# A bidirectional recurrent stack on one core: the first pair of items reordered, the fold of gamma and beta moved into other slots, late norms allowed to catch up

## The chip, the core and the metric

The kernel runs on one core of one Trainium2 chip. A core has TensorE (PE, matrix products and transposes into PSUM), VectorE (DVE), ScalarE (ACT), GpSimd (POOL) and SyncE (SP, which issues most DMAs here). Each engine works through its own queue in order and waits on semaphores for the others. The metric is the device time of one execution in microseconds; lower is better.

## The reference, cut to what matters

For each of B = 8 items, x is 512 tokens by 512 features. Layer norm, then a stack of four layers in two directions (the backward one over the reversed tokens, with the same weights), a fusion with a residual, then a feed-forward block with ternary weights and another residual:

```python
def _mingru(x, Wz, bz, Wh, bh):              # here Wz = Wh and bz = bh
    z = sigmoid(einsum('bsi,hi->bsh', x, Wz) + bz)
    h_tilde = tanh(einsum('bsi,hi->bsh', x, Wh) + bh)
    a = clip(1.0 - z, CLAMP_LO, CLAMP_HI)
    return _linear_scan(a, z * h_tilde)       # h[t] = a[t] * h[t-1] + b[t]

def _stack(x, ...):
    h = x
    for i in range(4):
        h_new = _mingru(h, Wz[i], bz[i], Wh[i], bh[i])
        if i > 0:
            h_new = h_new + h
        h = _layernorm(h_new, gamma, beta)
    return h

x = x + einsum(concat(stack_fwd(ln(x)), stack_bwd(ln(x))), fusion_W) + fusion_b
x = x + ffn(ln(x))     # W_fc and W_proj reduced to -1, 0, 1 by the mean of their magnitudes
```

The last layer's gamma and beta need not be applied to the states: fusion_W can be multiplied by gamma, the mean can be taken out of its rows, and beta's part goes into the bias. The kernel calls that the fold.

## The kernel before, in words

**Tiles.** The recurrent state of one item and direction lies with features on partitions: four chunks of 128 features by 512 tokens (`xT[b]`, `h_bd`). A layer of an item and direction is four *chunks* `u_bd_l_o`: a float32 product of four accumulating matmuls (eight in the trace, 128x512), then on ACT three activations of it (a, t and z; L431 to L433), on DVE the clamp and product (L437, L438), the scan over the tokens (L442) and the residual sum (L497). In the first layer both directions share the product: DVE scales u by the tokens' reciprocal deviation (L464), ACT makes a, t, z, and DVE runs a forward scan into `zf` and a backward scan into `z`.

**Norms.** Layer norm needs tokens on partitions. A *turn* `pt` (L293) is four 128x128 transposes on PE into a PSUM buffer, then statistics on DVE (L149 to L160), the power on POOL (L156), and a scaled copy to a token tile on ACT (`tok`, L166 and L167). After all four turns of a state a *back* `pf` (L302) transposes four token tiles into one chunk of the new state, and ACT copies it out with gamma and beta (L308). PSUM holds four buffers for u (`ps_u`), two for turns (`ps_t`) and two for backs (`ps_f`); a tile's buffer is free again after its last reader.

**Slots.** The order of work is written out by hand. `slot(work, cap)` issues one piece of PE work (a chunk, or a fusion tile), then what is due: first-layer scalings ("factors"), up to `cap` turns and backs from the queues `turns` and `backs` (`shares`), turns of x or y (`x_shares`), first-layer "scans", the work's own DVE end, "resid" stages, and then the ACT copies of the turns and backs. `now` counts slots. `extra` holds the work on the ternary weights: every second slot in the first pair (absolute values on ACT), every fourth later (comparisons on DVE, L171 and L172, with DMA in and out). `shares` takes a second piece when the slot's cap is 2, or when the piece is late: `late = at + piece < now`.

**Order of the run.** Items go in pairs. Before the loop: loads, statistics of x of item 0, the centring of the first weights (`pm0`), the first layers of items 0 and 1 (`f0`, `f1`). For each pair: layers 1 to 3 over (b,0), (b,1), (b+1,0), (b+1,1), then eight fusion tiles (`pu`, L528) with the next pair's first layers in between. The feed-forward block for all items comes last, from about 1,250 us.

**The fold before.** Behind the first layers two slots of their own form the sums over gamma and beta (`fold_sums`, PE chunk `pfold`, L609); behind (1,0) and (1,1) of layer 1 one slot each multiplies the four chunks of the fusion weights of one direction (`fold`: `pm` L625 on PE, four L630 on DVE), and one more slot adds to the bias (`fold_bias`: `pb` L636, L639).

Waits in the trace carry the line of a helper, so tiles are named here by item, direction, layer and chunk: `pt_10_0_2` is the turn of token block 2 for item 1, direction 0, layer 0.

Of the kernel before, what the change touches and what calls it, by code (L numbers as in the profile page):

```python
# [9 lines left out]
F32 = mybir.dt.float32  # L10
F32R = mybir.dt.float32r
AF = mybir.ActivationFunctionType
ALU = mybir.AluOpType
# [11 lines left out]
def kernel(  # L25
# [89 lines left out]
    warm = const.tile([P, 1], F32, name="warm")  # L115
    nc.vector.memset(warm, 0.0)

    xT[0] = hp.tile([P, NC_, S], F32, tag="h", name="xT_0")
# [4 lines left out]
    for c in range(NC_):  # L123
        (nc.scalar if c % 2 else nc.sync).dma_start(out=xT[0][:, c, :], in_=xt[0][ts(c, P), :])
    load_xT(1)
    for t in range(NT):
        load_x("n", 1, t)
    nc.sync.dma_start(out=gam, in_=gamma)
    nc.sync.dma_start(out=bet, in_=beta)
# [77 lines left out]
    with rec:  # L207
# [28 lines left out]
        def shares(cap):  # L236


            last = []
            for q in (turns, backs):  # L240
                some = []
                for i in range(2):
                    if not q or not ready(q[0][0]):
                        break
                    at, piece = q[0][:2]
                    late = (at.at if isinstance(at, Tokens) else at) + piece < now[0]
                    if i >= cap and not late:
# [39 lines left out]
        def turned(zs, t, name, frees=0):  # L287
            def source():
                if t == NT - 1:
                    zlive[0] -= frees  # L290
                pt = ps_t.tile([P, H], F32, tag="pt", name=f"pt_{name}")
                for c in range(NC_):
                    nc.tensor.transpose(pt[:, ts(c, P)], zs[c][:, ts(t, P)], ident)  # L293
                return pt
            return source
# [20 lines left out]

        def norm(s, zs, tag, pause):

# [125 lines left out]
        def first_layer(b, lag=0):  # L444
# [4 lines left out]
            def chunk(o):  # L449
                def work():  # L450
# [11 lines left out]
                    def scaled():  # L462
# [140 lines left out]


        def fold_sums(d):

            ps = ps_u.tile([P, H], F32, tag="u", name=f"pfold_{d}")
            for c in range(NC_):
# [3 lines left out]
                )  # L612

            def end():
                folded[d] = tokp.tile([P, H], F32, tag="tok", name=f"fold_{d}")
                held[0] += 1
                nc.scalar.copy(folded[d], ps)
            return end

        folded = {}  # L620

        def fold(d):

            pm = ps_u.tile([P, H], F32, tag="u", name=f"pm_{d}")
            nc.tensor.matmul(pm, lhsT=picks[1], rhs=folded[d], start=True, stop=True)  # L625

            def end():
                for c in range(NC_):
                    w = fw[:, d * NC_ + c, :]
                    nc.vector.scalar_tensor_tensor(w, w, gam[:, c : c + 1], pm, ALU.mult, ALU.subtract)  # L630
            return end

        def fold_bias():
            pb = ps_u.tile([P, H], F32, tag="u", name="pb")
            for d in range(2):
                nc.tensor.matmul(pb, lhsT=picks[0], rhs=folded[d], start=(d == 0), stop=(d == 1))  # L636

            def end():
                nc.vector.tensor_tensor(fb, pb, fb, ALU.add)  # L639
                held[0] -= 2  # L640
            return end

# [17 lines left out]
        take(xbacks)()  # L660
        both = const.tile([P, NC_, 2, 64], F32, name="both")
        picks = []
        for i in range(2):
            s = const.tile([P, P], F32, name=f"fpick{i}")
            nc.vector.memset(s, 0.0)
            nc.vector.memset(s[64 * i : 64 * i + 1, :], 1.0 / H if i else 1.0)
            picks.append(s)
        f0, f1 = first_layer(0), first_layer(1, 2)
        for work in f0:
            slot(work, 2)  # L670
        for i, v in enumerate((bet, gam)):
            nc.vector.tensor_copy(both[:, :, i, :], v.unsqueeze(2).broadcast_to([P, NC_, 64]))
        for work in f1:
            slot(work, 2)
        for d in range(2):
            slot(lambda d=d: fold_sums(d), 2)
        for b in range(0, B, 2):
# [13 lines left out]
            for l in range(1, L):  # L691
# [5 lines left out]
                for s in ((b, 0), (b, 1), (b + 1, 0), (b + 1, 1)):  # L697
# [258 lines left out]
```

## Time and profile before

| | us |
|---|---|
| median of 3 runs | 1767.56 |
| lowest and highest | 1766.42, 1767.7 |
| the profiled execution | 1769.31 |
| its span, first to last instruction | 1767.3 |
| busy: PE, DVE, ACT, POOL | 1721.4, 1451.1, 1066.2, 214.5 |

A busy share is an average over all stages. In the page's 40 slices (44 us each) PE is busy for 90% or more from the fourth slice on to the last but one, and its clock is granted at nine tenths or more in each slice; what happens inside the first 160 us is seen in windows of 20 us and in the timelines. The matrix products here are float32. PE's rows in a timeline overlap a little, since matmuls are pipelined; durations between starts are the safer measure.

### The profile page before, as it was taken

How to read it: one execution, taken by the hardware profiler on the slowest of the kernel's cores; microseconds unless marked ns; L12 is line 12 of the kernel's file. 1: busy time of each engine (PE TensorE's matmuls, PEld its weight loads, DVE VectorE, ACT ScalarE, POOL GpSimd, SP SyncE). 2: the span in 40 equal slices, each digit the busy share in tenths (PEclk: the TensorE clock that was granted, in tenths of full speed). 3: DMA queues.
4: the chain of work that ended last, by engine and by line, in shares of the span. 5: the costliest groups of instructions: out<-in, count | busy, mean ns of one | idle time of the engine just before them, and what ended most of it. 6: DMA issues, size and time to landing. Idle time of an engine off the chain costs nothing.

```text
span 1767.3 us, 19729 instructions
## 1 busy us (share of the span) xinstructions
PE 1721.4 (97%) x6424; PEld 1046.7 (59%) x6424; DVE 1451.1 (82%) x2865; ACT 1066.2 (60%) x1836; POOL 214.5 (12%) x334
## 2 busy tenths in 40 slices
PE   7989999999999999999999999999999999999998
PEld 3554554455554445555444455554588888888886
DVE  6977989779999977999897799997468778778876
ACT  2887884358886325787632588872156556566653
POOL 1111111111111111111111111111000000000000
PEclk9999999999999999999999999999999999999999
DMA  7002210110231111123101201101301101101100
GB/s 262 12 30 78 96 54 19 48 48 13 72 102 54 28 38 54 36 72 107 49 24 42 96 13 48 59 14 42 126 1 48 38 11 48 49 9 40 48 24 24
DMA packets 46454, 91.73 MB, mean 52 GB/s; under 512 B 5264, under 2 KB 5264, under 8 KB 45328
## 3 DMA queue, kind: packets, MB, share of 16 engines
q1 hardware_dynamic: 45488, 88.91, 14.8%
q10 hardware_dynamic: 864, 1.57, 0.3%
q8 instruction: 50, 0.82, 0.2%
q14 instruction: 52, 0.43, 0.1%
HBM read 65.30 MB, written 25.17 MB: 51 GB/s over the span
## 4 chain that ended last, share of the span: by engine, by line
PE 62%; DVE 29%; issue 6%; ACT 2%; POOL 0%; DVEq 0%; DMA 0%; POOLq 0%; ACTq 0%
PE u L414 16%; PE pu L528 12%; PE ph L782 12%; PE po L809 11%; DVE z L442 7%; DVE st L149 5%; DVE z L438 4%; PE u L457 4%; PE pt L293 3%; DVE z L497 2%; PE pf L302 2%; DVE a L437 2%; DVE mv L151 1%; DVE ve L155 1%; DVE st_x L149 1%
## 5 line engine op out<-in xcount | busy, mean ns | idle before, releaser
L414 PE MATMUL u<-xT,gw 128*128 128x512 f32 x768 | 351.1, 601 | 0.0
L414 PE MATMUL u<-h,gw 128*128 128x512 f32 x768 | 350.7, 600 | 0.0
L442 DVE TENSOR_TENSOR_SCAN z<-a,z 128x512 f32<-128x512 f32 x224 | 274.3, 1224 | 7.8
L149 DVE BATCH_NORM_STATS2 st<-pt 128x6 f32<-128x512 f32 x256 | 177.2, 692 | 71.7 <-PE pt L293 71.2
L786 ACT ACTIVATE g<-ph 128x512 f32<-128x512 f32 x128 | 76.4, 597 | 245.9 <-PE ph L782 245.9
L414 PEld LDWEIGHTS u<-xT,gw 128*128 128x128 f32 x768 | 141.2, 194 | 141.0 <-issue 141.0
L414 PEld LDWEIGHTS u<-h,gw 128*128 128x128 f32 x768 | 141.1, 194 | 140.7 <-issue 140.7
L156 POOL TENSOR_TENSOR rs<-ve,mhalf 128x1 f32<-128x1 f32 x192 | 122.9, 640 | 704.1 <-DVE nmu L160 649.1
L809 PE MATMUL po<-pwq,ghi 128*128 128x512 f32 x512 | 203.6, 398 | 0.0
L809 PE MATMUL po<-pwq,glo 128*128 128x512 f32 x512 | 199.9, 390 | 0.0
L782 PE MATMUL ph<-yhi,fcq 128*128 128x512 f32 x512 | 199.8, 390 | 0.0
L782 PE MATMUL ph<-ylo,fcq 128*128 128x512 f32 x512 | 199.7, 390 | 0.0
L431 ACT ACTIVATE a<-u,ngb 128x512 f32<-128x512 f32 x192 | 131.2, 683 | 99.6 <-PE u L414 98.7
L438 DVE TENSOR_TENSOR z<-z,t 128x512 f32<-128x512 f32 x224 | 153.7, 686 | 16.6 <-ACT z L433 16.6
L167 ACT ACTIVATE tok<-pt,nmr,rs 128x512 f32<-128x512 f32 x192 | 149.2, 777 | 6.4
L797 DVE TENSOR_TENSOR acc<-acc,g 128x512 f32<-128x512 f32 x112 | 77.4, 691 | 91.1 <-ACT g L786 90.1
L433 ACT ACTIVATE z<-u,gb 128x512 f32<-128x512 f32 x192 | 132.6, 691 | 0.0
L431 ACT ACTIVATE a<-z,ngb 128x512 f32<-128x512 f32 x32 | 23.1, 722 | 179.7 <-DVE z L464 179.7
L432 ACT ACTIVATE t<-u,gb 128x512 f32<-128x512 f32 x192 | 131.0, 682 | 0.0
L302 PE MATMUL pf<-ident,tok 128*128 128x128 f32 x768 | 116.8, 276 | 13.0 <-ACT tok L167 10.4
L293 PEld LDWEIGHTS pt<-ident,z 128*128 128x128 f32 x640 | 78.8, 142 | 84.6 <-issue 52.4
L166 ACT ACTIVATE nmr<-nmu,rs 128x1 f32<-128x1 f32 x192 | 56.5, 294 | 107.5 <-POOL rs L156 96.8
(138 smaller groups left out, 2711.0 us busy)
## 6 DMA issues: line engine op xcount, KB each, us to landing
xn<-in_x_dram SPq DMA_DIRECT2D x32, 256.0 KB, 4.6
xf<-in_x_dram SPq DMA_DIRECT2D x32, 256.0 KB, 4.3
x<-xf SPq DMA_DIRECT2D x32, 256.0 KB, 2.0
xy<-x SPq DMA_DIRECT2D x32, 256.0 KB, 4.1
out_dram<-xy SPq DMA_DIRECT2D x32, 256.0 KB, 2.0
xT<-in_xt_dram SPq DMA_DIRECT2D x7, 1024.0 KB, 7.0
fca<-in_fc_wT_dram SPq DMA_DIRECT2D x16, 256.0 KB, 2.9
pwa<-in_proj_wT_dram SPq DMA_DIRECT2D x16, 256.0 KB, 2.7
```

The costliest lines, as they stand in the source:

```text
L149: nc.vector.bn_stats(st, src)
L167: nc.scalar.activation(dst, src, AF.Identity, bias=nmr, scale=rs)
L293: nc.tensor.transpose(pt[:, ts(c, P)], zs[c][:, ts(t, P)], ident)
L302: nc.tensor.transpose(pf[:, ts(t, P)], toks[t][:, ts(c, P)], ident)
L414: nc.tensor.matmul(u, lhsT=gw[l][:, c, ts(o, P)], rhs=h[:, c, :], start=(c == 0), stop=(c == NC_ - 1),)
L431: nc.scalar.activation(a, u, AF.Sigmoid, bias=ngb[:, l, o : o + 1], scale=-1.0)
L433: nc.scalar.activation(z, u, AF.Sigmoid, bias=gb[:, l, o : o + 1])
L438: nc.vector.tensor_tensor(z, z, t, ALU.mult)
L442: nc.vector.tensor_tensor_scan(dst[:, d], a[:, d], z[:, d], 0.0, ALU.mult, ALU.add)
L528: nc.tensor.matmul(pu, lhsT=hs[d][:, c, ts(t, P)], rhs=fw[:, d * NC_ + c, :], start=(c == 0), stop=(c == NC_ - 1),)
L782: nc.tensor.matmul(ph, lhsT=w, rhs=ys[b][c][i], start=(c == 0 and i == 0), stop=(c == NC_ - 1 and i == 1),)
L809: nc.tensor.matmul(po[b][t], lhsT=part[:, ts(t, P)], rhs=pwq[k // NP_][:, k % NP_, :], start=(k == 0 and i == 0), stop=(k == NF - 1 and i ...
```

## The change

- The backward scan of the first layer of item 0 is put off to the "resid" stage of the next slot. Item 1's stay where they were.
- Before the first slot two of item 1's four x statistics are issued; the loads of its x are issued ahead of the load of `xT_1`.
- The slot of item 1's second chunk has a cap of 4: all four turns of item 0's forward norm go into it. The last two of those turns use the `ps_f` buffers. `shares` takes up to `cap` pieces.
- In the first pair's first-layer norms turns and backs are numbered in pairs (`t // pair`, `c // pair`), so that two of them are due per slot.
- A piece counts as late one slot earlier: `<=` for `<`. This holds for all pairs.
- The fold has no slots of its own. `fold_sums(d)` follows (0,0) and (0,1) of layer 1; `fold(d)` follows (0,0) and (0,1) of layer 2 and puts one chunk in each of four slots; `fold_bias` follows (1,0) of layer 2. There are five slots fewer, so the pieces of `extra` meet other chunks.
- The constants of the fold (`both`, `fpick`) are set up at the start.

```diff
     for c in range(NC_):
         (nc.scalar if c % 2 else nc.sync).dma_start(out=xT[0][:, c, :], in_=xt[0][ts(c, P), :])
-    load_xT(1)
     for t in range(NT):
         load_x("n", 1, t)
+    load_xT(1)
...
-                for i in range(2):
+                for i in range(max(2, cap)):
                     if not q or not ready(q[0][0]):
                         break
                     at, piece = q[0][:2]
-                    late = (at.at if isinstance(at, Tokens) else at) + piece < now[0]
+                    late = (at.at if isinstance(at, Tokens) else at) + piece <= now[0]
...
-                pt = ps_t.tile([P, H], F32, tag="pt", name=f"pt_{name}")
+                spare = name.startswith("00_0") and t > 1
+                pt = (ps_f if spare else ps_t).tile([P, H], F32, tag="pf" if spare else "pt", name=f"pt_{name}")
...
-        def norm(s, zs, tag, pause):
+        def norm(s, zs, tag, pause, pair=1):
...
-                queue(turns, s, at, t, tokens(turned(zs, t, f"{tag}_{t}", NC_), toks, None, f"{tag}_{t}"))
+                queue(turns, s, at, t // pair, tokens(turned(zs, t, f"{tag}_{t}", NC_), toks, None, f"{tag}_{t}"))
             for c in range(NC_):
-                queue(backs, s, toks, c, back(toks, dst, c, True, f"{tag}_{c}"))
+                queue(backs, s, toks, c // pair, back(toks, dst, c, True, f"{tag}_{c}"))
...
                             scan(f, a, z, False)
-                            scan(z, a, z, True)
                             zf.append(f)
-                            zb.append(z)
                             if o == NC_ - 1:
                                 state[b, 0] = xT.pop(b)
-                                norm((b, 0), zf, f"{b}0_0", 1)
-                                norm((b, 1), zb, f"{b}1_0", 1)
+                                norm((b, 0), zf, f"{b}0_0", 1, 2 if b < 2 else 1)
+
+                            def backward():
+                                scan(z, a, z, True)
+                                zb.append(z)
+                                if o == NC_ - 1:
+                                    norm((b, 1), zb, f"{b}1_0", 1, 2 if b < 2 else 1)
+                            if b == 0:
+                                stages.append((now[0] + 1, "resid", backward))
+                            else:
+                                backward()
...
-            def end():
-                for c in range(NC_):
+            for c in range(NC_):
+                def chunk(c=c):
                     w = fw[:, d * NC_ + c, :]
                     nc.vector.scalar_tensor_tensor(w, w, gam[:, c : c + 1], pm, ALU.mult, ALU.subtract)
-            return end
+                stages.append((now[0] + c, "resid", chunk))
...
+        for _ in range(2):
+            take(xturns)
         f0, f1 = first_layer(0), first_layer(1, 2)
-        for work in f0:
-            slot(work, 2)
+        for i, work in enumerate(f0 + f1):
+            slot(work, 4 if i == NC_ + 1 else 2)
         for i, v in enumerate((bet, gam)):
             nc.vector.tensor_copy(both[:, :, i, :], v.unsqueeze(2).broadcast_to([P, NC_, 64]))
-        for work in f1:
-            slot(work, 2)
-        for d in range(2):
-            slot(lambda d=d: fold_sums(d), 2)
...
-                    if s[0] == 1 and l == 1:
-                        slot(lambda d=s[1]: fold(d))
-                        if s[1] == 1:
-                            slot(fold_bias)
+                    if b == 0 and l == 1 and s[0] == 0:
+                        fold_sums(s[1])
+                    if b == 0 and l == 2:
+                        if s[0] == 0:
+                            fold(s[1])
+                        elif s[1] == 0:
+                            fold_bias()
```

More of the change, by code (lines that the diff above doesn't have):

```diff
@@ L116 @@
     nc.vector.memset(warm, 0.0)
+    both = const.tile([P, NC_, 2, 64], F32, name="both")
+    picks = []
+    for i in range(2):
+        s = const.tile([P, P], F32, name=f"fpick{i}")
+        nc.vector.memset(s, 0.0)
+        nc.vector.memset(s[64 * i : 64 * i + 1, :], 1.0 / H if i else 1.0)
+        picks.append(s)
     xT[0] = hp.tile([P, NC_, S], F32, tag="h", name="xT_0")
@@ L602, in combined @@
                 nc.vector.tensor_tensor(lo, v, hi.bitcast(F32), ALU.subtract)
+        folded = {}
         def fold_sums(d):
@@ L612, in fold_sums @@
                 )
-            def end():
-                folded[d] = tokp.tile([P, H], F32, tag="tok", name=f"fold_{d}")
-                held[0] += 1
-                nc.scalar.copy(folded[d], ps)
-            return end
-        folded = {}
+            folded[d] = tokp.tile([P, H], F32, tag="tok", name=f"fold_{d}")
+            held[0] += 1
+            nc.scalar.copy(folded[d], ps)
         def fold(d):
@@ L625, in fold @@
             nc.tensor.matmul(pm, lhsT=picks[1], rhs=folded[d], start=True, stop=True)
-            def end():
-                for c in range(NC_):
+            for c in range(NC_):
+                def chunk(c=c):
                     w = fw[:, d * NC_ + c, :]
                     nc.vector.scalar_tensor_tensor(w, w, gam[:, c : c + 1], pm, ALU.mult, ALU.subtract)
-            return end
+                stages.append((now[0] + c, "resid", chunk))
         def fold_bias():
@@ L636, in fold_bias @@
                 nc.tensor.matmul(pb, lhsT=picks[0], rhs=folded[d], start=(d == 0), stop=(d == 1))
[L638 to L641, printed above, removed]
+            nc.vector.tensor_tensor(fb, pb, fb, ALU.add)
+            held[0] -= 2
         def load_pair(use, b):
@@ L660 @@
         take(xbacks)()
[L661 to L667, printed above, removed]
+        for _ in range(2):
+            take(xturns)
         f0, f1 = first_layer(0), first_layer(1, 2)
-        for work in f0:
-            slot(work, 2)
+        for i, work in enumerate(f0 + f1):
+            slot(work, 4 if i == NC_ + 1 else 2)
         for i, v in enumerate((bet, gam)):
             nc.vector.tensor_copy(both[:, :, i, :], v.unsqueeze(2).broadcast_to([P, NC_, 64]))
-        for work in f1:
-            slot(work, 2)
-        for d in range(2):
-            slot(lambda d=d: fold_sums(d), 2)
         for b in range(0, B, 2):
```

## The prediction

> **What bounds the kernel now.** I read the busy shares first, then a table of windows over the first 200 us, then the timelines of TensorE (PE) and VectorE (DVE), and last the chain of work that ended last.
>
> ```profile
> PE 1721.4 (97%) x6424; PEld 1046.7 (59%) x6424; DVE 1451.1 (82%) x2865; ACT 1066.2 (60%) x1836; POOL 214.5 (12%) x334
> ...
> 20.00:40.00 20.00, 16.38 (x46) 7.86 (x45) 19.37 (x35) 6.17 (x9) 2.12 (x4) 0.96 0.69 251
> 40.00:60.00 20.00, 18.80 (x73) 10.21 (x71) 14.91 (x39) 16.80 (x30) 4.59 (x8) 0.95 0.01 1
> ...
> 140.00:160.00 20.00, 16.89 (x57) 8.80 (x56) 14.18 (x34) 12.88 (x26) 2.96 (x5) 0.83 0.09 27
> 160.00:180.00 20.00, 20.00 (x72) 10.50 (x71) 16.98 (x31) 16.69 (x32) 1.97 (x3) 1.00 0.40 135
> ```
>
> A window row gives its length, then busy us of PE, weight loads, DVE, ACT, POOL, then granted clock. PE is the bound over the whole span; only in the first pair is it short of work: 140 to 160 has 3.1 us idle and a clock of 0.83, the next window neither. The PE rows show where:
>
> ```profile
> 37.51 0.77 PE L293 MATMUL pt<-ident,zf 128*128 128x128 f32 x5 [3.51 <-DVE zf L442]
> ...
> 100.31 1.12 PE L302 MATMUL pf<-ident,tok 128*128 128x128 f32 x4 [2.58 <-ACT xT L308]
> ...
> 123.79 2.37 PE L293 MATMUL pt<-ident,z 128*128 128x128 f32 x8 [2.43 <-ACT tok L167]
> ...
> 139.90 3.60 PE L414 MATMUL u<-h,gw 128*128 128x512 f32 x8
> ...
> 151.91 0.48 PE L302 MATMUL pf<-ident,tok 128*128 128x128 f32 x1 [2.62 <-ACT tok L167]
> 152.18 6.42 PE L414 MATMUL u<-xT,gw 128*128 128x512 f32 x8
> ```
>
> Each wait costs its idle time and then a stretch at half clock: the chunk at 152.18 takes 6.42 us, the one at 139.90 takes 3.60 (3.44 from start to start). Idle plus slow work, worked out from the start times of PE's instructions: 3.7+1.8 at 37.5, 2.3+1.7 at 60, 0.6 at 88, 2.7+1.5 at 100, 2.6+1.9 at 124, 0.7 at 149, 2.8+3.0 at 152 and 0.3 at 34: 25.6 us between 13 and 158 us. What DVE does before the last two:
>
> ```profile
> 149.65 2.71 DVE L630 SCALAR_TENSOR_TENSOR fw<-fw,gam,pm 128x512 f32<-128x512 f32 x4
> 152.28 0.69 DVE L149 BATCH_NORM_STATS2 st<-pt 128x6 f32<-128x512 f32 x1
> ...
> 159.08 0.70 DVE L149 BATCH_NORM_STATS2 st<-pt 128x6 f32<-128x512 f32 x1 [4.97 <-PE pt L293]
> ```
>
> The slots that only fold give PE a matmul of 1 us, DVE 2.71 us, and no chunk to cover it. Later the same coupling shows once per pair:
>
> ```profile
> 596.55 1.10 issue
> 597.65 0.68 DVE xT L503
> 598.85 4.86 PE u L414 x8
> ```
>
> Here the quantiser (the "issue" row, its 0.48+0.75 us on DVE) sits just ahead of a residual sum that PE awaits: 3.1 us idle, 1.6 slow; the same at 908.
>
> **Durations.** From the DVE timeline, start to start: scaling M 0.70, product P 1.06, scan S 1.25, residual R 0.70, one norm turn N 1.13 (its token 2.9 after its start: 38.63 to 41.55). A layer slot is P+S+R+N = 4.1 on DVE, and 3.44 + 2 x 0.44 = 4.31 on PE.
>
> **Part by part: the first layer.** The order of the instructions on each engine in the changed program, walked with these durations. Two x1 statistics (1.05 each) move ahead of the first M. Their loads are issued ahead of xT_1's on SP's queue, about 8.2 to 10, and land some 6 us later, when DVE gets there (14.4). xT_1 is issued last of the five; it is first read at 26, so 4 us later costs nothing. The memsets (0.7 us) move into the DMA wait at the start: nothing. With the backward scans a slot behind, zf_0_0_3 ends at 35.9 instead of 37.5. All sixteen transposes of 00_0 follow, but the scale transpose pr_1 now needs a buffer of ps_f, and both hold turns: it waits for tok_00_0_2. DVE runs N from 37.2 (after one backward scan), the third at 39.5, its token at 42.4. So PE idles 4.3 us, u_1_0_2 starts at 43.0 (before: 38.9) and ends, partly slow, at 48.2. Behind it stand pt_01_0_0 and the turns 01_0, queued on DVE ahead of item 1's scaling: DVE idles 1.2 + 4.0 + 2.2 us up to 54. From there DVE has no break: two N (56.3), P S S (59.9), the two copies into both (0.5), M, P S S (64.6), slot 00_1_0 (67.6), M, P S S (71.9), slot 00_1_1 (74.9), P and the forward scan of 1_0_3: 77.2. PE goes u_1_0_3 53.4, u_00_1_0 58.6, and 62.9, 67.2, 70.7 for the next three (chunks of 3.44, groups of four transposes of 0.44 between them), then waits for that scan 6.5 us, and 1.8 slow. pfold_0 ends at 83.2, the chunks of 01_1 at 86.6, 90.9, 96.1, 101.3 (0.4 of waits for token buffers), pfold_1 106.5, u_10_1_0 110.0 (DVE waits 2.4 for it), then 4.31 a slot, once 0.4 for a token behind ACT: u_00_2_0 ends at 146.0. POOL's order stays the same; on ACT scale_1 now stands behind four tokens (1.08 each), which is the 1.2 above. Its losses are 2.9 + 6.3 + 8.6 + 0.8 = 18.6 us. The other way round: before, u_00_2_0 ends at 158.6 with 5.2 us more done (pm, pm, pb, four groups): 158.6 - 5.2 - 146.0 = 7.4. **Gain 25.6 - 18.6 = 7.0 us**, most of it from the waits at 100, 124, 149 and 152.
>
> [...]
>
> **Folding.** The two pfold sums (3.44 each) leave slots of their own, where they covered DVE's scans, for layer 1; pm and pb (0.86, 0.86, 1.72) go to layer 2. PE's sum is unchanged, and the walk contains them. DVE's eight fw pieces (2.71/4 = 0.68 each) go one to a slot of layer 2: 4.1 + 0.68 = 4.8 against 4.31, for eight slots, plus fb 0.68: 6.1 us more on DVE, less 0.2 x 8 of slack, less 3.4 that PE itself gains there. Left: 1.1, and PE waits for the last token of a norm, where I find 0.6 us of slack in the old order. Bounds: 0 (hidden by DVE's tenth of idle between 160 and 250) and 6.1 plus two slow stretches. I take **-1.5**. pm holds one of four ps_u buffers for four slots; three are enough, since a chunk's three ACT readers (2.1 us) end within a slot.
>
> **Five slots fewer.** The quantiser's pieces (1.23 us of DVE, one per four slots) shift by two pieces and to other chunks. In pair two 5 instead of 7 precede the wait at 551 (2.6 us): +1.2. Up to the awaited sum at 598 there are then three instead of two: -1.2; the same at 908: -1.2. Pair four gets two more in layer 1: -0.3. The small threshold steps now fall into layer 3 of pair one, where DVE is late (wait at 294): -0.5. **Sum -2.0.** ACT's absolutes and the fca and pwa loads keep their spacing; they are not waited for.
>
> **Late turns.** With <= and up to two, in the three fusion stages a turn (1.13) moves one slot of 10.75 us earlier, three turns and four backs in each. There PE waits 0.3 + 1.45 (at 661 and 669, and again 971 and 980) for token buffers, with a quantiser piece ahead of those turns; after the shift it is elsewhere. Bounds +2.9 and -3 (one extra N per fusion slot ahead of the sums that free ps_u). I take **+1.0**.
>
> **Sum:** 7.0 - 1.5 - 2.0 + 1.0 = 4.5 us. The profiled execution took 1769.31 (span 1767.3), 1.75 above the median of the runs, so I take it off the median: 1767.56 - 4.5 = 1763.0. Some 0.2%, or 3.5 us, is what a measurement here can tell from no change.
>
> **The rivals.**
> - *The cover is better than I think* (0.15): layer 2 takes fw for nothing, 551 gains and 598 loses less, fusion gains 2: 1759. For it: DVE busy 17.0 of 20 at 160 to 180. Against it: DVE ends the chain all through pair two.
> - *Spent later* (0.12): quantiser and late turns cost 4.5 together; 7.0 - 1.5 - 0.5 - 4.5 = 0.5: 1767. This includes a change without effect.
> - *Folding makes DVE the bound of layer 2* (0.18), slower: if a layer slot has no slack on DVE, its 6.1 us come out as PE waits, two of them long enough for slow work (1.7 each): 9.5 instead of 1.5, with the late turns' +1.0 lost: 7.0 - 9.5 - 2.0 = -4.5: 1772. It decides from the point where P no longer waits for ACT in those slots. For it: 149.65, where 2.71 us on DVE became 2.62 idle and 3.0 slow. Against it: one piece at a time, with a chunk of 3.44 to cover it.
>
> **Chances.** My forecast has 0.55, with its own range 1758 to 1767, of which 0.33 lies below 1764.0 and 0.22 within 0.2%. So faster 0.33 + 0.15 = 0.48, same 0.22 + 0.12 = 0.34, slower 0.18. The range takes in the better rival and most of the third.
>
> **What would show it.** Right: PE idle about 4 us before pr_1 near 42 and about 6.5 before pt_10_0_0 near 77, none over 1 us from 90 to 150, u_00_2_0 finished near 146; a small wait in 180 to 215; the wait at 598 and 908 longer by 1. Wrong: slow work at 100 to 150, waits over 2 us in layer 2, or a first stage where PE doesn't wait for pr_1.

## The result and the profile after

| | us, median | runs | lowest to highest |
|---|---|---|---|
| before | 1767.63 | 10 | 1766.15 to 1769.26 |
| after | 1763.91 | 10 | 1759.61 to 1765.73 |

The ratio is 0.9975, with a 95% interval of 0.9967 to 0.9984: 3.7 us less. On a second chip it was 0.9974 (0.9966 to 0.9982). The profiled execution of after was among the two lowest of its ten: 1759.63 us, span 1757.6, mean granted clock 0.995, where five of the ten had 0.992. That of before stood 1.7 us above its median, at 0.990. So the two spans differ by 9.7 us, and only 3.7 of it is the change in the medians. A second profile of after, from a run nearer its median (label e5_after, span 1762.5, clock 0.992), stands beside it below.

The busy line of the profile page of after:

```profile
PE 1710.4 (97%) x6424; PEld 1042.0 (59%) x6424; DVE 1450.2 (83%) x2865; ACT 1067.4 (61%) x1836; POOL 216.2 (12%) x334
```

The counts are those of before, and PE is still the bound. Its 11 us less of busy time are not less work: most of them, some 9 us by the granted clocks of the two profiles (0.990 of 1767.3 us, 0.995 of 1757.6), are fewer matmuls at half clock. The table of windows (length, busy us of PE, weight loads, DVE, ACT, POOL, then granted clock) shows where the waits of the first pair are now:

```profile
40.00:60.00 20.00, 19.55 (x73) 11.35 (x74) 11.11 (x28) 14.76 (x26) 3.52 (x5) 0.86 0.00 1
60.00:80.00 20.00, 15.15 (x44) 6.95 (x43) 19.55 (x26) 13.24 (x23) 0.00 (x0) 0.91 0.09 26
...
140.00:160.00 20.00, 20.00 (x74) 10.76 (x73) 18.38 (x39) 18.02 (x34) 3.53 (x5) 1.00 0.45 145
```

140 to 160, which had 3.1 us idle at a clock of 0.83, is full at 1.00. What is left of the first pair's waits stands between 34 and 80. PE's timeline there (start, us, what, and in brackets the idle time before it and who ended it):

```profile
33.87 1.64 PE L301 MATMUL pt<-ident,zf 128*128 128x128 f32 x13 [1.54 <-DVE zf L450]
40.45 1.08 PE L352 MATMUL pr<-ident,rx 128*128 128x128 f32 x4 [4.94 <-ACT tok L174]
41.33 5.74 PE L465 MATMUL u<-xT,gw 128*128 128x512 f32 x8
...
62.71 1.32 PE L310 MATMUL pf<-ident,tok 128*128 128x128 f32 x8 [0.97 <-ACT h L316]
75.11 0.77 PE L301 MATMUL pt<-ident,zf 128*128 128x128 f32 x5 [3.87 <-DVE zf L450]
75.71 5.30 PE L626 MATMUL pfold<-fw,both 128*128 128x512 f32 x8
...
140.23 3.60 PE L422 MATMUL u<-xT,gw 128*128 128x512 f32 x8
```

pr_1 waits 4.94 us for a token's release of its buffer, and the chunk behind it runs partly at half clock (5.74 against 3.60). The turn pt_10_0_0 waits 3.87 for the forward scan, and pfold_0 behind it is slow too (5.30). From 95 to 204 us there is no wait over 0.2 us. DVE pays for the buffer as well:

```profile
42.79 0.69 DVE L472 TENSOR_TENSOR z<-u,scale 128x512 f32<-128x512 f32 x1 [1.99 <-ACT scale L356]
47.55 0.70 DVE L156 BATCH_NORM_STATS2 st<-pt 128x6 f32<-128x512 f32 x1 [4.06 <-PE pt L301]
52.73 0.70 DVE L156 BATCH_NORM_STATS2 st<-pt 128x6 f32<-128x512 f32 x1 [2.21 <-PE pt L301]
```

**A ledger for all kernels.** From the start times of PE's instructions: the next one starts 0.43 us behind a matmul of 512 columns and 0.11 behind a transpose (medians 0.429 and 0.109 in before and in after), and what exceeds that is counted as lost time; in the MLP, where the median step is 0.23, only what exceeds 0.38 is. An excess of one such step again (0.3 to 0.46, or about 0.11) is counted as work at half clock; the rest is idle. The idle part of after repeats from one execution to the other (44.4 and 44.2); the half-clock part does not (5.9 and 10.8). The clocks in the traces give a check on the half-clock part: apart from the last microseconds, before ran at half clock for 9 stretches of 3.41 us, after for 4, and e5_after for 7. With PE at work through all of it, a stretch loses half of itself, 1.7 us, so 15.4, 6.8 and 11.9; the ledger's column is off from such counts by up to 2.3 us. Idle us by stage in the profiled execution: first pair to 210, to 440 (rest of pair one), to 1260 (pairs two to four), whole; then half clock, whole:

| kernel | us | before beside it | ratio, 95% interval | to 210 | to 440 | to 1260 | idle | half clock |
|---|---|---|---|---|---|---|---|---|
| before | 1767.63 | | | 18.9 | 3.2 | 22.1 | 45.5 | 14.6 |
| after | 1763.91 | 1767.63 | 0.9975 (0.9967 to 0.9984) | 14.1 | 3.6 | 24.7 | 44.4 | 5.9 |
| e5_after | 1764.08 | 1768.02 | 0.9974 (0.9966 to 0.9982) | 14.2 | 3.6 | 24.6 | 44.2 | 10.8 |
| e1_fold_alone | 1752.70 | 1765.11 | 0.9936 (0.9923 to 0.9950) | 10.7 | 2.2 | 21.1 | 35.8 | 7.6 |
| e2_fold_slots | 1766.85 | 1765.11 | 1.0007 (1.0000 to 1.0014) | 19.5 | 3.3 | 23.8 | 48.0 | 11.7 |
| e3_late_first | 1757.40 | 1765.11 | 0.9964 (0.9952 to 0.9977) | 15.0 | 3.5 | 22.5 | 42.6 | 8.2 |
| e4_scale_first | 1756.69 | 1765.11 | 0.9952 (0.9939 to 0.9966) | 10.4 | 3.5 | 24.5 | 40.1 | 5.4 |
| e6_two_slots | 1761.34 | 1768.02 | 0.9965 (0.9952 to 0.9977) | 13.0 | 3.9 | 22.8 | 41.5 | 10.1 |
| e7_backward_now | 1761.54 | 1768.02 | 0.9966 (0.9953 to 0.9978) | 15.3 | 3.6 | 24.2 | 45.0 | 7.1 |
| e8_phase | 1757.73 | 1768.02 | 0.9948 (0.9935 to 0.9960) | 13.8 | 3.5 | 21.7 | 41.1 | 6.2 |
| e9_all | 1752.61 | 1768.11 | 0.9915 (0.9901 to 0.9928) | 10.9 | 3.6 | 21.6 | 37.0 | 5.7 |
| e10_all_later | 1757.50 | 1768.11 | 0.9940 (0.9927 to 0.9952) | 10.5 | 3.5 | 24.6 | 40.1 | 8.1 |
| e11_fold_early | 1753.68 | 1768.11 | 0.9920 (0.9906 to 0.9933) | 11.5 | 2.3 | 21.3 | 36.7 | 5.1 |
| e12_all_late_first | 1753.94 | 1768.11 | 0.9916 (0.9903 to 0.9930) | 10.2 | 3.6 | 22.2 | 37.8 | 7.2 |

The runs were on several chips, whose times of before differ by 3 us (1765.11 to 1768.11), so kernels of different chips are compared by their difference from before. The ledger closes: before and after lose 60.1 and 50.3 us, a difference of 9.8 for spans 9.7 apart. In idle time the change wins 1.1 us in all: 4.8 in the first pair, of which pairs two to four give back 2.6. The rest of the 3.7 is half-clock work. All runs together say the same. A run's span times its mean granted clock is taken as an estimate of its time without the half-clock part. Averaged over the runs this is 1749.6 to 1749.7 for before on each of three chips (so what differs between these chips is, by this estimate, the half-clock part), 1748.9 to 1749.0 for after, 1742.4 for the folding alone, 1745.9 for e8_phase and 1750.8 for e7_backward_now. It is good to about 1 us where there are five runs, since the clock is listed to 0.001. By it the change wins 0.7 us.

### The profile page after: what moved, and what is told of

Its sections match the earlier page's. It is cut to its first block, busy times and chain, and to the rows that moved or that the text cites. A ratio compares the mean times of both kernels' runs of the same rounds, so it can differ in the third digit from the quotient of the medians.

```text
span 1757.6 us, 19731 instructions
## 1 busy us (share of the span) xinstructions
PE 1710.4 (97%) x6424; PEld 1042.0 (59%) x6424; DVE 1450.2 (83%) x2865; ACT 1067.4 (61%) x1836; POOL 216.2 (12%) x334
## 4 chain that ended last, share of the span: by engine, by line
PE 62%; DVE 30%; issue 6%; ACT 2%; DMA 1%; POOL 0%; DVEq 0%; POOLq 0%; ACTq 0%
PE u L422 16%; PE ph L784 12%; PE po L811 11%; PE pu L543 11%; DVE z L450 8%; DVE st L156 5%; DVE z L446 4%; PE u L465 4%; PE pt L301 3%; PE pf L310 2%; DVE a L445 2%; DVE z L512 2%; DVE mv L158 1%; DVE ve L162 1%; DVE zf L450 1%
## 5 line engine op out<-in xcount | busy, mean ns | idle before, releaser
L422 PE MATMUL u<-xT,gw 128*128 128x512 f32 x768 | 345.4, 593 | 0.0
L310 PE MATMUL pf<-ident,tok 128*128 128x128 f32 x768 | 113.0, 273 | 6.4 <-ACT tok L174 5.4
```

The source lines that it names most:

```text
L310: nc.tensor.transpose(pf[:, ts(t, P)], toks[t][:, ts(c, P)], ident)
L422: nc.tensor.matmul(u, lhsT=gw[l][:, c, ts(o, P)], rhs=h[:, c, :], start=(c == 0), stop=(c == NC_ - 1),)
```

## The experiments

My theory was that the gain comes from the folding, and that the reordered first layers, the late rule and the shifted quantiser win little or cost something (A). The rival was that the reordered first layers carry it (B).

**The folding alone**

```diff
--- before
-        for d in range(2):
-            slot(lambda d=d: fold_sums(d), 2)
...
-                    if s[0] == 1 and l == 1:
-                        slot(lambda d=s[1]: fold(d))
+                    if b == 0 and l == 1 and s[0] == 0:
+                        fold_sums(s[1])
+                    if b == 0 and l == 2:
+                        if s[0] == 0:
+                            fold(s[1])
...
```

> The kernel before with the folding part alone: no slots of its own for the fold, the fw pieces one to a slot of layer 2, the constants made at the start. First layers, their turns and the late rule stay as before. Theory A (the fold carries the gain): the waits at 149 and 152 (0.7 + 2.8 + 3.0 us) go and one of the two at 100 and 124 (4.2 or 4.5) becomes smaller; layer 2 costs 1.0 and the shifted quantiser about 2. So 3 to 6 us less than before: 1762 to 1765. Theory B (the reordered first layers carry it): the waits at 37.5, 60 and 100 stay and the freed ones are taken up by the next waits: within 1.5 us of before, 1766 to 1769.

12.4 us less than before, over three times what the whole change brings. PE's waits in the first pair, from its timeline:

```profile
36.45 1.33 PE L301 MATMUL pt<-ident,zf 128*128 128x128 f32 x5 [3.51 <-DVE zf L450]
51.38 0.66 PE L301 MATMUL pt<-ident,z 128*128 128x128 f32 x4 [2.72 <-ACT tok L175]
68.73 0.33 PE L301 MATMUL pt<-ident,zf 128*128 128x128 f32 x1 [1.46 <-DVE zf L450]
...
151.48 1.04 PE L301 MATMUL pt<-ident,z 128*128 128x128 f32 x8
```

All four waits of before at 100, 124, 149 and 152 are gone (15.2 us with their half-clock work), where I had expected the last two and a part of a third to go; the turns at 151.48 now wait for nothing. In layer 2 the fw pieces cost nothing that the ledger shows: the stretch to 440 has 1.0 us less idle than before. The direction is A's, the size at least twice the 3 to 6 us that A gave. So the other parts of the change cost what separates this kernel from after: 12.4 - 3.9 = 8.5 us by the times, 44.2 - 35.8 = 8.4 by idle time: 3.5 in the first pair, 1.4 up to 440 and 3.5 in pairs two to four. This kernel has four slots fewer than before, a whole period of the quantiser's pieces, so here the pieces stay where they were; in after, with six fewer, they do not.

**The fold in slots again**

```diff
--- after
+        for d in range(2):
+            slot(lambda d=d: fold_sums(d), 2)
...
-                    if b == 0 and l == 1 and s[0] == 0:
-                        fold_sums(s[1])
...
+                    if s[0] == 1 and l == 1:
+                        slot(lambda d=s[1]: fold(d))
...
```

> The kernel after with the fold in its five slots again, all else as after. Theory A: the fold's slots bring back the waits of 2.7 + 3.0 us and 0.7 near their end, and the two pfold slots leave DVE behind: 3 to 6 us more than after, 1767 to 1770, no better than before. Theory B: the reordered first layers keep what they won: 1764 to 1765, as after.

1.7 us above before on the same chip, where after is 3.9 below on another: B falls. The reordered first layers without the folding win nothing (19.5 us idle to 210, 18.9 before). It is no clean addition, since the fold's place right behind the first layers brings a wait of its own. PE's timeline:

```profile
59.45 6.74 PE L624 MATMUL pfold<-fw,both 128*128 128x512 f32 x8 [5.00 <-DVE both L682]
```

pfold waits for the copies into both, which stand on DVE behind the scans of item 1.

**The late rule in the first pair alone**

```diff
--- after
-                    late = (at.at if isinstance(at, Tokens) else at) + piece <= now[0]
+                    late = (at.at if isinstance(at, Tokens) else at) + piece < now[0] + ahead[0]
...
                 pace[0] = 4
+                ahead[0] = 0
```

> The kernel after, with the rule that lets a late norm catch up by two taken in the first pair alone; from the second pair on a turn is late only when it is a whole slot behind, as before. Theory A (the rule wins nothing later: the wait of 1.47 us for a turn's buffer stood at 647 as at 669 before, and one of 1.64 came at 694): 0.5 to 1.5 us less than after, 1762.5 to 1763.5. Theory B, the prediction's: the rule saves 1.0 there, so 1765.

Against before 7.7 us less, by the ratio 0.9964; after has 0.9974, and the intervals overlap, so the times alone do not settle it. In idle time the pairs two to four lose 22.5 us without the rule and 24.6 to 24.7 with it: at this place of the quantiser's pieces the rule costs 2.1 us. Span times granted clock gives the same difference (1746.8 and 1748.9). That is A's side and more than A said.

**The scale ahead of the four turns**

```diff
--- after
-            last = shares(cap) + x_shares()
+            last = x_shares() + shares(cap) if scale_first else shares(cap) + x_shares()
...
-            slot(work, 4 if i == NC_ + 1 else 2)
+            slot(work, 4 if i == NC_ + 1 else 2, i == NC_ + 1)
```

> The kernel after with one thing moved: in the slot of the four turns, item 1's scale transpose pr_1 and the copy of its scale stand ahead of the turns, on PE and on ACT. pr_1 then needs no buffer that a turn holds. Theory A (PE's 4.94 us before pr_1 and DVE's idle 2.0 + 4.1 + 2.2 us are one wait for that buffer): the wait of 7.7 us at 40 shrinks to under 2, DVE reaches the forward scan of 1_0_3 some 6 us earlier, and the 4.1 + 1.7 at 75 goes too: 7 to 11 us less than after, 1753 to 1757. Theory B (the wait only moves on: DVE's norms and scans are what the first stage waits for, whatever stands first): PE waits as long at 01_0's turns instead, and the time is within 2 us of after.

8.4 us under before. The idle time to 210 falls from 14.1 to 10.4. PE's timeline:

```profile
34.45 1.64 PE L301 MATMUL pt<-ident,zf 128*128 128x128 f32 x13 [1.10 <-DVE zf L450]
35.92 3.60 PE L465 MATMUL u<-xT,gw 128*128 128x512 f32 x8
...
41.42 0.77 PE L301 MATMUL pt<-ident,z 128*128 128x128 f32 x5 [1.57 <-DVE z L450]
...
70.27 0.77 PE L301 MATMUL pt<-ident,zf 128*128 128x128 f32 x5 [3.87 <-DVE zf L450]
```

The wait for the buffer is gone, and 1.8 us at 41 and 0.6 at 43 take its place. The wait for the forward scan keeps its 3.87 us and only comes 4.8 us earlier: DVE got there sooner, but so did PE. So A is right on the first half and wrong on the second, and the size, 4.5 below after by the differences from before, lies between A and B.

**After once more**

> The kernel after itself, unchanged, on the chip of the next three, so that they are compared with it there. Both theories: 3 to 6 us less than before, as in its first runs (3.7).

3.9 us less than before (14 runs), as expected.

**Item 0's turns in two slots**

```diff
--- after
-                spare = name.startswith("00_0") and t > 1
-                pt = (ps_f if spare else ps_t).tile([P, H], F32, tag="pf" if spare else "pt", name=f"pt_{name}")
+                pt = ps_t.tile([P, H], F32, tag="pt", name=f"pt_{name}")
...
-            slot(work, 4 if i == NC_ + 1 else 2)
+            slot(work, 2)
```

> The kernel after with item 0's first turns in two slots of two, in the two buffers of ps_t alone, all else as after. Theory C (the four turns in one slot are what makes the first layers lose: pr_1 waits 4.94 us for a buffer that a turn holds): pr_1 no longer waits, the 7.7 us at 40 become the shorter wait for a token, and the time falls 3 to 6 us below after. Theory D (the turns in one slot win, and only pr_1's place spoils it): the second two turns come a slot of 3 to 4 us later, the first chunk of 00_1 waits for them, and the time is 0 to 4 us above after.

6.7 us under before, 2.7 under after on the same chip. PE's timeline has the waits for tokens that I expected, and none at pr_1:

```profile
41.06 0.66 PE L300 MATMUL pt<-ident,zf 128*128 128x128 f32 x4 [1.25 <-ACT tok L174]
...
50.70 2.11 PE L300 MATMUL pt<-ident,z 128*128 128x128 f32 x8 [2.78 <-ACT tok L174]
```

To 210 that is 1.2 us less idle than after (13.0 against 14.2); another 1.8 comes in pairs two to four, because this kernel takes a slot more and the quantiser's pieces fall elsewhere. C has the direction, with less in it than it claimed: as after has them, the four turns in one slot lose 1.2 us net. D's time is missed, but not its mechanism. The kernel with the scale first keeps the four turns in one slot and has no wait at pr_1 either, and it is idle for 10.4 us to 210, 2.6 less than this one. So the four turns in one slot win, and pr_1's place takes more than that away.

**Backward scans beside the forward ones**

```diff
--- after
-                            if b == 0:
-                                stages.append((now[0] + 1, "resid", backward))
-                            else:
-                                backward()
+                            backward()
```

> The kernel after with item 0's backward scans beside the forward ones again instead of a slot behind, all else as after. If the deferral wins what the prediction gave it: zf_0_0_3 ends a scan of 1.25 us later, the wait of 1.7 us at 34 becomes 3, perhaps with 1.7 of slow work behind it: 1 to 3 us above after. If it wins nothing, because the same scan then stands later between the norms and 01_0's turns: within 1 us of after.

PE's timeline:

```profile
35.47 1.64 PE L301 MATMUL pt<-ident,zf 128*128 128x128 f32 x13 [2.44 <-DVE zf L450]
42.20 1.08 PE L352 MATMUL pr<-ident,rx 128*128 128x128 f32 x4 [5.10 <-ACT tok L174]
```

The wait for zf_0_0_3 grows from 1.54 to 2.44, and to 210 this kernel is 1.1 us more idle than after: that is what the deferral wins. The time is 2.5 us lower than that of after all the same, which neither expectation had. All five runs had a clock of 0.995, which only 3 of the 14 of after on this chip had: the difference is in half-clock work (7.1 and 10.8 us in the profiles), and by span times granted clock this kernel is 1.9 us longer than after. Why these runs had less of it is not settled.

**The quantiser's pieces two slots later**

```diff
--- after
-            if extra and now[0] % pace[0] == 0:
+            if extra and (now[0] + pace[0] // 4 * 2) % pace[0] == 0:
```

> The kernel after with the quantiser's pieces two slots later from the second pair on, where the pairs start at slots 72, 136 and 200 instead of 78, 142 and 206. Theory E (six slots fewer moved the pieces by two in their period of four, ahead of the residual sums that PE awaits): 0.6 at 570 and 878 goes and 3.6 at 590 and 898 becomes 3.1 as before, 2.2 us in all, and the waits of 1.5 and 2 us in the fusion stages move by some tenths: 1.5 to 3 us below after. Theory F (the longer waits there come from the turns of the late rule, not from the pieces): 0.6 and 3.6 stay, within 1 us of after.

10.3 us under before and 6.4 under after, on one chip: more than E had. In the idle time it is 3.1 in all, 2.9 of it in pairs two to four; the rest is half-clock work (6.2 against 10.8 in the profiles). The waits of 0.6 at 570 and 878 are gone and those at 590 and 898 are down from 3.6 to 3.1, as E said (the one before 542 grows by 0.4); those of the fusion stages fall from 1.47 and 1.64 to 0.81 and 0.46 at 647 and 694, and from 1.47, 0.67 and 2.08 to 0.81, 0.67 and 0.87 at 956 to 1004. F falls. In the chain of waits of after the piece stands between two residual sums; the second one ends PE's wait:

```profile
578.53 0.67 DVE xT L518
...
579.63 0.75 DVE fcq L179
...
589.38 0.59 DVE xT L518
...
590.02 0.33 PE pt L301
```

DVE has no break there, so its 1.2 us come out at 590. Two more pieces lie between PE's last wait at 542 and that one, at 543.1 and 559.8; in this kernel and in before there are two in all. On DVE's timeline of this kernel the next piece comes right behind the awaited sum, where it costs nothing:

```profile
588.78 0.67 DVE L518 TENSOR_TENSOR xT<-z,xT 128x512 f32<-128x512 f32 x1
589.36 0.48 DVE L178 TENSOR_SCALAR fcq<-fcb,lo_fc 128x512 f32<-128x512 f32 x1
589.88 0.75 DVE L179 SCALAR_TENSOR_TENSOR fcq<-fcb,hi_fc,fcq 128x512 f32<-128x512 f32 x1
```

**Three moves together**

```diff
--- after, with the scale first and the pieces two slots later
+                def with_fold(work=work):
+                    end = work()
+                    fold_sums(0)
+                    return end
+                slot(with_fold if s == (0, 0) and l == 1 and o == NC_ - 1 else work)
...
```

> The kernel after with three moves: pr_1 and its scale ahead of the four turns, the quantiser's pieces two slots later from the second pair on, and the sum pfold_0 issued right behind the chunk u_00_1_3, ahead of the turn pt_10_0_0 that waits for the forward scan. Theory G (the three add up): in the first pair 0.6 us is left of the 4.0 at 70 and its slow 1.7 goes, the other waits stay as in the kernels with one move; 4.4 (scale) + 6.4 (pieces) + about 4 (pfold_0) under after, so 13 to 18 us under before. Theory H (DVE bounds the first pair, so that PE's 3.4 us of work done earlier come back as a wait behind it): pt_10_0_0 waits for less, the first turns of 10_0 or the chunks of 01_1 wait for more; 10 to 13 us under before.

15.5 us under before, inside the span of G; but what G says of pfold_0 is wrong. PE's timeline:

```profile
66.61 3.60 PE L632 MATMUL pfold<-fw,both 128*128 128x512 f32 x8
...
70.98 0.77 PE L301 MATMUL pt<-ident,zf 128*128 128x128 f32 x5 [0.44 <-DVE zf L450]
71.58 3.60 PE L422 MATMUL u<-h,gw 128*128 128x512 f32 x8
78.06 0.66 PE L301 MATMUL pt<-ident,zf 128*128 128x128 f32 x4 [2.88 <-ACT tok L174]
```

pfold_0 now covers the wait for the scan (0.44 left of 3.87), and the next turns wait 2.88 and 0.59 for tokens, whose statistics DVE reaches only after two more scans. To 210 the kernel is idle 10.9 us, no less than the 10.4 in the one with the scale first and pfold_0 in its old place: DVE is the limit here, as H has it. The gain is that of the scale and of the pieces.

**The pieces three slots later**

```diff
--- the three moves
-            if extra and (now[0] + pace[0] // 4 * 2) % pace[0] == 0:
+            if extra and (now[0] + pace[0] // 4) % pace[0] == 0:
```

> The same three moves with the quantiser's pieces three slots later than in after instead of two, the one place in their period of four that no run has had. Theory E (a piece costs where it stands ahead of a residual sum or a turn that PE awaits): the waits at 540 to 700 and 850 to 1010 differ again by tenths to 1.2 us each; the residual sum of the wait near 590 has two pieces of the layer ahead of it in this place, so 3.1 there and no 0.6 before it, and the sum within 1.5 us of the two-slot kernel. Theory F (the place matters only by the turns of the late rule): no difference between the two, within 0.3 us.

4.9 us above the three moves, with 3.0 more idle in pairs two to four: the place matters (F falls), but the waits are 0.60 at 566 and 3.63 at 586, not E's 3.1, although just two pieces stand between the waits at 537 and 586. So the count of pieces does not explain this place, and what does stays open. My text is also wrong that no run had it: counted from the start of a pair (slot 72, 73, 74, 77 or 78), the first piece comes in slot 3 here and in the two kernels whose pairs start at 73 and 77, in slot 2 in before and in the best kernels, in slot 0 in after. Their idle time in pairs two to four is 22.8 to 24.6, 21.1 to 22.2, and 24.6 to 24.7. Slot 1 was not run.

**pfold_0 earlier in the kernel with the folding alone**

```diff
--- the folding alone
...
+                slot(with_fold if s == (0, 0) and l == 1 and o == NC_ - 2 else work)
...
```

> The kernel with the folding part alone, with pfold_0 a slot and a half earlier as well: right behind the chunk u_00_1_2, ahead of the turn that waits 1.5 us for the forward scan of 1_0_3 near 69. Theory G: that wait goes and nothing takes its place: 1 to 2.5 us below the folding alone, which was 12.4 under before on its chip, so 13.5 to 15 under before. Theory H: 1.6 us come back as a wait for a norm's token before 100, so 12 to 13 under before.

14.4 us under before, within G's span; the folding alone was 12.4 under on another chip, and the intervals overlap. The idle time says H: the wait at 69 is gone, but with 0.45 at 79, 0.9 at 88 and a wait of 1.0 for a copy at 57 it comes to 11.5 to 210, against 10.7. The gain in the times, if there is one, is not idle time.

**The three moves with the late rule in the first pair alone**

> The three moves together, with the rule that lets a late norm catch up by two in the first pair alone. With the pieces at their old place the rule of later pairs should matter less than at after's place, where the waits at 647 and 956 were 1.47 with it and 0.96 without. Theory A (the rule wins nothing later): within 1 us of the three moves with the rule, on either side, the waits near 650 and 960 moving by 0.6 or less. The prediction's view: the rule saves about 1 us there, so 0.5 to 1.5 us slower without it.

1.3 us above the three moves, at 0.9916 against 0.9915: no difference that the times show. PE's timelines at the turn that waits for its buffer, first of the three moves, then without the later rule:

```profile
656.12 0.66 PE L301 MATMUL pt<-ident,z 128*128 128x128 f32 x4 [0.58 <-ACT tok L174]
```

```profile
656.19 0.66 PE L302 MATMUL pt<-ident,z 128*128 128x128 f32 x4 [0.67 <-ACT tok L174]
657.18 0.66 PE L302 MATMUL pt<-ident,z 128*128 128x128 f32 x4 [0.34 <-ACT tok L174]
```

There the rule takes 0.64 us off each of two fusion stages and adds 0.66 at 992: 0.6 in all (21.6 against 22.2). So its sign hangs on the place of the pieces: it gains 0.6 here and costs 2.1 in after.

The three moves, at 0.9915, beat both before and after (0.9974 or 0.9975). The folding alone with pfold_0 earlier, 0.9920, and the three moves without the later rule can't be told from them.

## Why the prediction was right, and which steps were not

The predicted 4.5 us stand against 3.7 (3.9 on the second chip), and the direction was right. The sum hides errors of both signs, and its closeness is partly luck. It charges each wait with a fixed piece of half-clock work. In the two profiles of after that work differs by 5 us (4 and 7 stretches at half clock) with the same waits, which is more than the whole forecast; the last section shows why.

- *The first pair, 7.0.* Idle and half-clock work from 12.3 to 210 were 26.2 us and are 17.8 in one profile of after and 19.2 in the other: 8.4 and 7.1. The walk was right in its places too. pr_1 does wait for tok_00_0_2: 4.9 to 5.1, predicted 4.3. DVE's breaks were predicted as 1.2, 4.0 and 2.2 and are 1.99, 4.06 and 2.21. u_00_2_0 starts at 140.2 and so ends near 143.8, predicted 146.0. Mis-sized was the wait for the scan of 1_0_3, 3.9 instead of 6.5. A wait of 1.0 at 62.7 for a copy into the state was not in the walk.
- *Where it comes from.* The prediction put most of the 7.0 on the waits at 100, 124, 149 and 152. The runs show more: the folding alone takes all four away and is worth 12.4, and the other parts give back 8.5. In the first pair that is 3.5 us of idle time (14.2 against 10.7). The four turns in one slot lose 1.2 net, pr_1's place alone loses more (3.7), and the deferral wins 1.1; the earlier statistics, the place of the copies into both, the numbering in pairs and the late rule inside the first pair were not run alone, so how the 3.5 divides among all of them is open.
- *Short of work only in the first pair.* This reading was false. The ledger has before idle for 18.9 us in the first pair and for 22.1 in pairs two to four, and there the change loses.
- *Folding in layer 2, -1.5.* Too large. PE waits 0.45 at 204 and nothing before; the kernel with the folding alone has no wait there. The price of a slower layer slot was not paid because each piece finds DVE with time to spare, one to a chunk: from 165 to 201 us, with all eight of them, DVE is busy for 34.50 of 36 us, and PE for all 36. The third rival, which had DVE as the bound of layer 2, falls with it.
- *Fewer slots, -2.0.* The program has six fewer, not five: pair two starts at slot 72 instead of 78. The term for 598 and 908 was right: three pieces instead of two, and 3.6 with 0.6 ahead of it instead of 3.1, which is 1.1 each for 1.2. The gain of 1.2 at 551 did not come (2.6 us before and after), nor the loss at the threshold steps (1.9 us in both). By the kernel that only moves the pieces their place costs 2.9 us of idle time in pairs two to four, and half-clock work besides; but that is with the late rule on. One reading behind this step was false: the "issue" row ahead of the sum at 597.65 is not the quantiser. DVE's timeline of before has it behind that sum:

```profile
597.65 0.67 DVE L503 TENSOR_TENSOR xT<-z,xT 128x512 f32<-128x512 f32 x1
598.24 0.48 DVE L171 TENSOR_SCALAR fcq<-fcb,lo_fc 128x512 f32<-128x512 f32 x1
598.75 0.75 DVE L172 SCALAR_TENSOR_TENSOR fcq<-fcb,hi_fc,fcq 128x512 f32<-128x512 f32 x1
```

  The row is most of the scan at 596.51. before had its pieces in the better place by chance, and the change moved them out of it.
- *Late turns, +1.0.* This is the step that failed. In after the waits at 647 and 694 are 3.1 us where before had 1.9 (669 and 704), those at 956 to 1004 are 4.2 where before had 2.6. Before's small waits behind them (0.3 to 0.5 us at 735, 753 and 1047) are gone, so over the two fusion stretches as a whole (605 to 850 and 915 to 1165 us in before) after idles only some 0.8 us more. The rule itself costs 2.1 with the pieces where after has them. With them two slots later it gains 0.6. The prediction took the two steps apart, and they are not apart. The idle us of pairs two to four, with the first piece in slot 2 or in slot 0 of a pair:

| | slot 2 | slot 0 |
|---|---|---|
| no late rule there | 21.1 to 22.2 (before, e1, e11, e12) | 22.5 (e3) |
| late rule | 21.6, 21.7 (e8, e9) | 24.2 to 24.7 (after, e4, e5, e7) |

  Either alone changes little; the two together cost 2 us or more. That the turn which the rule takes earlier lands beside a piece would explain it, but no run singles that out.

So -1.5 for layer 2 was too dark, +1.0 for the late turns too bright, and the first pair about right: the errors cancelled.

## What to carry to other kernels

A slot whose PE work is short and whose DVE work is long (here 1.02 us for pm and 2.71 us for the four pieces) shifts the whole queue behind it, and the bill comes several waits later; spread such work one piece to a chunk. Work that is dealt out by a counter ("every fourth slot") is moved by any change in the number of slots: pin its place to the wait that it must not stand ahead of. And when a change has several parts, run each part alone: here one part won 12.4 us and the others gave back 8.5. Run together, too, the parts that meet on one engine: the late rule and the place of the pieces cost little each, and 2 us or more together.

## What the hardware showed

The half-clock work behind a wait is not fixed by the wait. The wait near 590, in the two executions of after, PE's timeline:

```profile
590.02 0.33 PE L301 MATMUL pt<-ident,xT 128*128 128x128 f32 x1 [3.42 <-DVE xT L518]
590.18 3.60 PE L422 MATMUL u<-h,gw 128*128 128x512 f32 x8
```

```profile
591.99 0.33 PE L301 MATMUL pt<-ident,xT 128*128 128x128 f32 x1 [3.41 <-DVE xT L518]
592.16 5.30 PE L422 MATMUL u<-h,gw 128*128 128x512 f32 x8
```

The same wait, and the chunk behind it takes 3.60 us in one and 5.30 in the other. The records of the granted clock show what differs. In all fourteen profiles it changes only on a grid of 3.413 us (in after at 38.81, 45.63, 76.35, 79.77, 898.97, 902.38 and 1752.30 us), and the grid lies differently against the program in each execution: the wait's end at 590.02 in after stands between marks at 588.35 and 591.77, its end at 591.99 in the second profile between marks at 589.91 and 593.32. Windows cut along this grid, at the same wait, first in after and then in its second profile (length, busy us of PE, weight loads, DVE, ACT, POOL, then granted clock):

```profile
584.94:588.35 3.41, 1.66 (x7) 0.65 (x5) 3.34 (x5) 2.12 (x4) 0.00 (x0) 1.00 0.00 0
588.35:591.77 3.41, 1.75 (x5) 0.93 (x6) 3.27 (x7) 0.00 (x0) 0.64 (x1) 1.00 0.00 0
591.77:595.18 3.41, 3.41 (x12) 1.72 (x11) 3.24 (x7) 1.32 (x2) 0.21 (x2) 1.00 0.02 5
```

```profile
589.91:593.32 3.41, 1.33 (x4) 0.74 (x5) 3.24 (x8) 0.00 (x0) 0.22 (x1) 1.00 0.00 0
593.32:596.74 3.41, 3.41 (x5) 1.35 (x4) 3.24 (x7) 0.90 (x2) 0.44 (x1) 0.50 0.03 5
```

In the first, the grid splits the wait into 1.75 and 1.66 us of idle time; in the second, one window holds 2.08 us of it, and the next window runs at half clock. Of all windows at full clock between 13 us and the last 12 us of the fourteen profiles, some 7,000, 49 had PE idle for 2.05 us or more, and all 49 were followed by one at half clock; before and after have 10 of them, from 2.10 us (before, 96.42) to 3.29 (after, 35.39). Of the 17 with 1.78 to 1.97 us 4 were (1.82 at 58.87 in before was, 1.86 at 847.77 in after was not), and none with less. A window at half clock was followed by another when PE idled over 0.66 us in it (11 of 11; 0.88 at 151.03 in before, 1.65 at 38.81 in after), and else by full clock (53 of 53). Transposes counted as work here: the first of these two windows of after held 16 of them and almost nothing else, with 1.54 us idle, and the clock stayed at 1.00 in the next.

```profile
31.98:35.39 3.41, 1.87 (x17) 1.51 (x14) 3.38 (x4) 0.00 (x0) 0.00 (x0) 1.00 0.54 194
35.39:38.81 3.41, 0.12 (x2) 0.00 (x0) 2.83 (x13) 1.72 (x4) 1.29 (x3) 1.00 0.01 2
```

So within the lengths seen here it was partly chance whether the clock halved behind a wait. Over the fourteen profiles, the waits of PE and those with half clock behind:

| length of the wait, us | waits | with half clock behind |
|---|---|---|
| 0.9 to 2.2 | 57 | 2 |
| 2.2 to 2.75 | 29 | 11 |
| 2.75 to 3.3 | 23 | 15 |
| 3.3 to 3.8 | 19 | 13 |
| over 3.8 | 13 | 12 |

In both of the two short ones a second wait shared the window (in before 1.22 us up to 60.03 and 0.67 up to 61.02). So a wait of 2.75 to 3.3 us cost its length and, in 15 of 23 cases, half-clock work besides: some 1.7 us for one stretch, which is what the chunk at 592 shows, and more where two stretches follow each other (6.42 us instead of 3.60 for the chunk at 152 in before). Of the waits under 2.2 us 2 of 57 did. That also explains the spread of after, 1759.6 to 1765.7 at clocks of 0.995 to 0.992, while the idle time of its two profiles is 0.2 us apart: one profile tells the idle time to some tenths, but the half-clock part only to several us.
